# A windowed attention and gated expert kernel: another opening for TensorE's instruction stream, another order in the first six steps, and one batch for the last four rows

## The chip, the cores and the metric

The kernel runs on one core of a Trainium2 chip. The metric is the device time of one execution in microseconds. Of the kernel before, three executions were timed: 4324.14, 4325.08 and 4339.78 us, with the median 4325.08. The profile comes from a further execution.

Five engines work side by side, each with its own instruction stream: PE (TensorE, matrix multiplies; PEld is its loading of weights), DVE (VectorE), ACT (ScalarE), POOL (GpSimd) and SP (SyncE, which here issues the transfers). They wait for each other through semaphores.

## The reference

The input `x` is two images of 128 channels and 256 x 256 pixels in 32-bit floats. Cut to what matters, the reference computes:

```python
x = x + conv_ref(ln_c(x))        # attention in windows of 8 x 8 pixels
t = to_tokens(x)                 # one token of 128 channels per pixel
t = t + ffn_ref(ln_t(t))         # experts
x = from_tokens(t, x)

# conv_ref: q, k, v by one 128 -> 384 product; each 8 x 8 window of q looks at
# a 12 x 12 window of k and v; relative position terms from q; a fixed mask
# that leaves one pixel in four; softmax; an output product
# ffn_ref: gate = softmax(x @ router_w + router_b); the best 2 of 8 experts,
# their gates divided by their sum; sum of gate * (x @ expert_w[e] + expert_b[e])
```

The mask parts the pixels into four parity planes (even and odd rows and columns) that have nothing to do with each other in the attention. `ln_c` and `ln_t` norm every pixel over its 128 channels.

## The kernel before

**Tiles.** Channels lie on the 128 partitions. The images are cut into 64 strips of 8 image rows (32 to an image). A strip has four planes, 512 pixels each, and four "rows" of two image rows, also 512 pixels each. A row (i, k) is row k of strip i.

**Steps.** One loop runs over n (L811). Step n computes the attention of plane n (strip n // 4), prepares plane n + 1, and does the experts for rows of the strip before. There are 256 planes; the loop has 263 turns, the last seven of which only drain the experts. The pieces of a step are generators, and the loop body takes one portion of a generator at a time: the order of the calls in the body is the order of the instructions on each engine. Inside `tc.manual_schedule` nothing is moved.

- `scores` (L464): products of `keys` with `au` (position terms, L476), then of `kcol` with `qs` (L493), then the exponential on ACT (L501).
- `attend` (L505): the sums of the exponentials (L514), called "the sums" here, the weighted values `av` (L524), and on DVE `sT`, `rc`, `rT` and `o` (L534 to L544), which divide.
- `out_project` (L548): `po` (L552) from `o`, and `xv` (L557), which adds it to the plane in place.
- `project` (L399), called `ahead` in the loop: values `pv` (L349) and `pu` (L408), the transposes and shifts that make `au` (L385 to L412), `pk` (L422) with ACT's copies to `kcol` (L433, L443), and `pq` (L447) with ACT's copy to `qs` (L449).
- `norms` (L565): ACT squares a row (L576), PE sums it over the channels in `plt` (L582), DVE works out the inverse deviation. It serves two rows at once: f, whose experts follow, and c, a row of a later strip (`row_at`, L761) that is to be normed for the attention. From n = 249 on there is no c, and the steps 250 to 255 are called short.
- `route` (L608): DVE picks two of eight gates per pixel. `spread` (L650): DVE's transpose makes `gT`, and SP sends it to a memory tile `gd` in two transfers (L661).
- `Experts`: `fetch` (L682) brings one expert's gates, spread over all partitions, in a transfer of 256 KB into one of eight `gb` tiles; `fetch_means` brings the mean term `sb`; `means` (L701) forms `xs`; `times` (L707) multiplies by a gate on DVE or POOL to give `xe`; `product` (L716) adds one expert's matrix product to `acc`; `end` (L722) adds `acc` to the row. `store` (L749) writes the row out.
- `first_norms` (L282) does the statistics of the first seven rows before the loop, in groups of four and three, and `ln1` (L273) norms them.

**Rooms.** Products go through three banks `ps_mm`, one bank `ps_acc` for `acc`, and four banks `ps_att` for the attention. The pool `xpool` has six strips.

**Instructions of PE.** `nc.tensor.addr_align(256, offset=157)` (L825) stands ahead of the scores of every step from 6 to 255. It asks for empty instructions until the next one has slot 157 of a block of 256. With `max_nops=0` the same call gives a branch over the space instead. PE fetches its program in blocks of 256 instructions; these fetches appear in the trace as the traffic of an instruction queue. A float32 product is four instructions, two loads of weights and two multiplies; a transpose is two.

**The start.** The loads of the first two strips are issued first, then the weights. Then DVE and PE prepare the weights: means taken off, four transposes `pw` (L166), the relative position tables (L176 to L190) and their product `wrel` (L195). Behind these in the order come the first statistics (L292), the projections of plane 0, and the loop.

Of the kernel before, what the change touches and what calls it, by code (L numbers as in the profile page):

```python
# [19 lines left out]
E = 8  # L20
# [23 lines left out]
KR, KC = 6, 10  # L44
NK = KR * KC
SLOT = 64
BLOCK, FIRST_LIMIT = 256, 99
NU = 9


@with_exitstack
def kernel(
# [39 lines left out]
    def mm_tile(name):  # L92
        return ps_mm.tile([P, 512], F32, tag="mm", name=name)

    def ctile(shape, name):
        return const.tile(shape, F32, tag=name, name=name)


    nc.scalar.preload_act_table_set("natural_log_exp_and_others")


    strips = [(b, s) for b in range(B) for s in range(NS)]
# [2 lines left out]
    def load_x(i, k, paced=False):  # L105

        if i >= len(strips):
            return
        b, s = strips[i]
        if k == 0:  # L110
            xt[i] = xpool.tile([P, R, W], F32, tag="xt", name=f"xt{i}")
        r = s * R + 2 * k
        if paced:
            nc.scalar.copy(xt[i][:, 2 * k, 0:1], onesm[:, 0:1])
        nc.sync.dma_start(xt[i][:, 2 * k : 2 * k + 2, :], x[b, :, r : r + 2, :])
# [22 lines left out]
    for j in range(4):  # L138
# [14 lines left out]
    nc.sync.dma_start(ew, expert_w.rearrange("e d c -> d e c"))  # L153
    nc.sync.dma_start(eb, expert_b.rearrange("e c -> (e c)").partition_broadcast(P))
    load_x(2, 0)

    wmean = ctile([P, 3, 1], "wmean")
    nc.vector.tensor_reduce(wmean, wall[:, 0:3, :], AX.X, ALU.add)
    nc.vector.tensor_scalar_mul(wmean, wmean, 1.0 / C)
    nc.vector.tensor_tensor(  # L160
        wall[:, 0:3, :], wall[:, 0:3, :], wmean.broadcast_to([P, 3, P]), ALU.subtract
    )
    wt = ctile([P, 4, P], "wt")
    pw = mm_tile("pw")
    for j in range(4):
        nc.tensor.transpose(pw[:, j * P : (j + 1) * P], wall[:, j, :], ident)  # L166
    nc.vector.tensor_copy(wt.rearrange("p j c -> p (j c)"), pw)
    nc.vector.tensor_scalar_mul(wt[:, 0, :], wt[:, 0, :], SCALE)
    wq, wk, wv, wo = (wt[:, j, :] for j in range(4))

    relT = []
    for rname, rsb in zip(("relh", "relw"), relsb):
        pr = mm_tile(f"p_{rname}")
        nc.tensor.transpose(  # L176
            pr[:, :n_rel], rsb.rearrange("r h d -> r (h d)"), ident[:n_rel, :n_rel]
        )
        rT = ctile([P, n_rel], f"{rname}T")
        nc.vector.tensor_scalar_mul(rT, pr[:, :n_rel], SCALE)  # L180
        relT.append(rT)
    mid = n_rel // 2
    lo = mid - 2 * (PR - 1)
    relbd = ctile([P, P], "relbd")
    nc.gpsimd.memset(relbd, 0.0)
    for h in range(HEADS):
        hp = slice(h * DH, (h + 1) * DH)
        for j in range(2):
            c0 = h * DH + NU * j
            nc.vector.tensor_copy(  # L190
                relbd[hp, c0 : c0 + NU], relT[j][hp, lo : lo + 2 * NU - 1 : 2]
            )
    wrel = ctile([P, P], "wrel")
    pr = mm_tile("p_wrel")
    nc.tensor.matmul(pr[:, :P], lhsT=wall[:, 0, :], rhs=relbd, start=True, stop=True)  # L195
    nc.vector.tensor_copy(wrel, pr[:, :P])

    xn, vwin, vrows, kcol = [], [], [], []
    zero = ctile([P, KR, P], "zero")
# [362 lines left out]
    for g in gboth:  # L562
        nc.gpsimd.memset(g, 0.0)

    def norms(f, c, nm):  # L565

        g = gboth[next(g_turn) % len(gboth)]  # L570
        srcs = []
        for j, src in ((0, f and rows_of(*f)), (2, c and ln1_src(*c))):
            if src is None:
                continue
            sq = work.tile([P, CH], F32, tag=f"sq{j}", name=f"sq{j}{nm}", bufs=1)
            nc.scalar.activation(sq, src, AF.Square)  # L576
            srcs += [(j, src), (j + 1, sq)]
        yield
        plt = mm_tile(f"plt{nm}")
        for j, src in srcs:  # L580
            for t in range(NT):
                nc.tensor.matmul(  # L582
                    plt[32 * t : 32 * t + 32, :P],
                    lhsT=rw[:, j],
                    rhs=src[:, t * P : (t + 1) * P],
                    start=(j == srcs[0][0]),
                    stop=(j == srcs[-1][0]),
                )
        yield
        plg = mm_tile(f"plg{nm}")  # L590
        nc.vector.transpose(plg[:, :P], plt[:, :P])
        p4 = plg[:, :P].rearrange("p (t e) -> p t e", e=32)
        k0, k1 = (0 if f else 1), (2 if c else 1)
        r, u = rstd(p4, plg[:, P : P + 2 * NT], k0, k1, nm)
        rs = None
        if f:
            rs = small.tile([P, NT], F32, tag="rs", name=f"rs{nm}")
            nc.vector.scalar_tensor_tensor(rs, u[:, 0], 3.0, r[:, 0], ALU.add, ALU.mult)
        if c:
            nc.vector.scalar_tensor_tensor(  # L600
                g[:, 1, :, 1], u[:, 1 - k0], 3.0, r[:, 1 - k0], ALU.add, ALU.mult
            )
        yield g, rs, p4
# [121 lines left out]
    class NoExperts:  # L725
# [18 lines left out]
        def end(self):  # L744
            pass

    to_store = []

    def store(i, k):  # L749
# [5 lines left out]

    n_planes = 4 * len(strips)

# [9 lines left out]

    first = [(0, k) for k in ln_rows(0)] + [row_at(n) for n in (-2, -1) if row_at(n)]
    parts = [first_norms(first[j : j + 4], f"n{j}") for j in range(0, len(first), 4)]
    for _ in range(3):
        for part in parts:
            next(part)
    if len(strips) > 1:
# [31 lines left out]

    ET = mybir.EngineType
    with tc.manual_schedule(engines={ET.PE, ET.DVE, ET.Activation, ET.Pool, ET.SP}):  # L810
        for n in range(n_planes + 7):  # L811
            i, pl = divmod(n, 4)
            score, attn, outp, ahead, norm, rout = none, none, none, none, none, none
            if n < n_planes:
                score = scores(n, states[n])
                attn = attend(n, states[n])
                outp = out_project(n, states[n])
            if n + 1 < n_planes:
                states[n + 1] = {}
                ahead = project(n + 1, states[n + 1])  # L820

            if 6 <= n < n_planes:
                nc.tensor.addr_align(BLOCK, offset=BLOCK - FIRST_LIMIT)  # L825


            next(score, None)
            new, row = NoExperts(), None
            if gated and gated[0]:  # L830
                rout = route(*gated[0], *gated[2])
            next(rout, None)
            nxt.fetch(5, nc.scalar)
            for _ in rout:
                pass
            next(score, None)
            next(ahead, None)
            nxt.fetch(7, nc.scalar)
            if gated:
                f, c, made = gated  # L840
                gd = spread(f, c, made[0], f"_{n}")
                new = Experts(*f, gd) if f else new
            if n + 1 < n_planes:
                send_values(n + 1, states[n + 1]["sent"])
            if gated and c:
                row = (*c, fetch_rstd(gd, f"_{n}"))
            next(ahead, None)
            if n + 1 < n_planes:
                states[n + 1]["shift"]()
            next(ahead, None)  # L850
            next(ahead, None)
            for e in (4, 6, 7, 5):
                ex.product(e)


            f = (i - 1, pl) if 0 < i <= len(strips) else None
            c = row_at(n)
            if f or c:
                norm = norms(f, c, f"_{n}")
            next(norm, None)  # L860
            next(attn, None)
            nxt.means()
            new.fetch_means()
            if n + 1 < n_planes:
                take_values(n + 1)
            for e in (0, 1, 2, 3):
                nxt.times(e, dve)
            new.fetch(0, dve)
            for e in (4, 6):
                nxt.times(e, dve)  # L870
            new.fetch(1, dve)
            ex.end()
            new.fetch(2, dve)
            next(attn, None)
            next(attn, None)


            ex = nxt
            next(norm, None)
            load_x((n + 9) // 4, (n + 9) % 4, paced=True)  # L880
            new.fetch(3, dve)
            while to_store:
                store(*to_store.pop())
            next(ahead, None)
            ex.product(0)
            made = next(norm, None)
            ex.product(1)
            ex.product(2)
            new.fetch(4, nc.scalar)
            nxt.behind(6)  # L890
            nxt.times(5, pool)
            if row:
                ln1(*row, pool)
            if pl == 3 and i + 2 < len(strips):
                halo(i + 2)
            nxt.times(7, pool)
            if n + 2 < n_planes:
                borders(n + 2)
            next(outp, None)
            ex.product(3)  # L900
            next(outp, None)
            new.fetch(6, dve)
            gated, nxt = (f, c, made) if made else None, new
            states.pop(n, None)

def shape_constants():

# [56 lines left out]
```

## Time and profile before

| | |
|---|---|
| median of three executions | 4325.08 us |
| profiled execution, its own time | 4331.68 us |
| its span, first to last instruction | 4329.9 us |
| mean granted clock of PE | 0.991 |
| busy: PE, DVE, ACT, POOL | 97%, 88%, 30%, 25% |
| first statistics on PE (L292) begin | 11.67 us |
| keys of step 0, of step 6, of step 7 begin | 28.71, 124.89, 143.88 us |
| median of a step from 7 to 248 | 16.24 us |
| keys of step 249, of step 255 begin | 4122.65, 4239.45 us |
| last `xv` (L557, step 255) begins | 4253.34 us |
| empty instructions, all ahead of keys | 8123 |

The times in the table are read from the timeline, which lists each engine's work in the order of its start. A step is taken from the start of its keys on PE (L476) to that of the next. In the busy table a share is of the span. In the stretches' table each row is one piece of time with the busy time of each engine in it and the mean granted clock of PE; 1.00 is the full clock. An idle time is shown in brackets, with what ended it; "issue" means that the profile shows no engine or transfer that was waited for.

### The profile page before, as it was taken

How to read it: one execution, taken by the hardware profiler on the slowest of the kernel's cores; microseconds unless marked ns; L12 is line 12 of the kernel's file. 1: busy time of each engine (PE TensorE's matmuls, PEld its weight loads, DVE VectorE, ACT ScalarE, POOL GpSimd, SP SyncE). 2: the span in 40 equal slices, each digit the busy share in tenths (PEclk: the TensorE clock that was granted, in tenths of full speed). 3: DMA queues.
4: the chain of work that ended last, by engine and by line, in shares of the span. 5: the costliest groups of instructions: out<-in, count | busy, mean ns of one | idle time of the engine just before them, and what ended most of it. 6: DMA issues, size and time to landing. Idle time of an engine off the chain costs nothing. (4 is left out here: it accounts for less than half of the span.)

```text
span 4329.9 us, 224393 instructions
## 1 busy us (share of the span) xinstructions
PE 4220.6 (97%) x94273; PEld 2464.3 (57%) x94273; DVE 3790.8 (88%) x11850; ACT 1320.4 (30%) x3774; POOL 1087.9 (25%) x1126
## 2 busy tenths in 40 slices
PE   7899999999999999999999999999999999999987
PEld 5455555555555555555555555555555555555553
DVE  5798898898888889988889889898888898888877
ACT  3223333332333333233332333333323232333321
POOL 1222222222222222222222222222222222222211
PEclk9999999999999999999999999999999999999999
DMA  4787878788787877878788787887878788787865
GB/s 112 212 245 241 248 236 246 241 244 248 235 239 240 247 236 248 248 235 251 240 247 241 243 247 238 247 248 239 247 233 246 233 250 244 239 246 239 245 190 190
DMA packets 824578, 1022.17 MB, mean 236 GB/s; under 512 B 137634, under 2 KB 409634, under 8 KB 823594
## 3 DMA queue, kind: packets, MB, share of 16 engines
q1 hardware_dynamic: 822864, 1007.52, 76.5%
q8 instruction: 769, 12.60, 1.3%
q14 instruction: 215, 1.76, 0.1%
q10 hardware_dynamic: 730, 0.29, 0.0%
HBM read 863.78 MB, written 143.75 MB: 233 GB/s over the span
## 5 line engine op out<-in xcount | busy, mean ns | idle before, releaser
L716 PE MATMUL acc<-xe,ew 128*128 128x512 f32 x4096 | 1918.4, 601 | 20.7 <-DVE gb L690 14.5
L716 PEld LDWEIGHTS acc<-xe,ew 128*128 128x128 f32 x4096 | 758.4, 190 | 940.3 <-issue 872.7
L707 DVE TENSOR_TENSOR xe<-xs,gb 128x512 f32<-128x512 f32 x1536 | 950.4, 685 | 11.2 <-PE acc L716 1.6
L711 POOL COPY last<-xe 128x1 f32<-128x1 f32 x256 | 47.6, 186 | 3120.0 <-DVE gb L690 3110.9
L707 POOL TENSOR_TENSOR xe<-xs,gb 128x512 f32<-128x512 f32 x512 | 652.1, 1275 | 1.5 <-PE att L524 1.0
L493 PE MATMUL att<-qs,kcol 32*60 32x32 f32 x32768 | 395.3, 223 | 16.7 <-issue 15.9
L493 PEld LDWEIGHTS att<-qs,kcol 32*60 32x60 f32 x32768 | 390.3, 127 | 21.1 <-issue 20.5
L275 POOL TENSOR_TENSOR xn<-xt,rb 128x512 f32<-128x512 f32 x249 | 374.0, 1502 | 93.5 <-DMA rb<-gd 92.7
L524 PEld LDWEIGHTS att<-pT,vwin 64*32 64x32 f32 x32768 | 349.7, 105 | 47.2 <-issue 9.3
L524 PE MATMUL att<-pT,vwin 64*32 64x32 f32 x32768 | 348.4, 200 | 6.5 <-issue 5.5
L501 ACT ACTIVATE pT<-att 128x1024 f32<-128x1024 f32 x256 | 262.2, 1024 | 296.3 <-PE att L493 296.3
L349 PE MATMUL pv<-wt,xn 128*128 128x128 f32 x2048 | 301.9, 291 | 0.9 <-issue 0.9
L412 DVE STREAM_TRANSPOSE uT<-pu 128x512 f32<-128x512 f32 x256 | 183.5, 717 | 132.1 <-PE pu L408 127.2
L576 ACT ACTIVATE sq<-xt 128x512 f32<-128x512 f32 x505 | 292.6, 630 | 0.0
L396 DVE STREAM_TRANSPOSE au<-auT 128x512 f32<-128x512 f32 x256 | 269.7, 1053 | 9.0
L552 PE MATMUL po<-o,wt 128*128 128x512 f32 x512 | 266.4, 602 | 10.2 <-DVE o L544 6.6
L408 PE MATMUL pu<-xn,wrel 128*128 128x512 f32 x512 | 267.5, 604 | 0.9 <-issue 0.9
L433 ACT COPY kcol<-pk 128x560 f32<-128x560 f32 (+2 forms) x344 | 183.4, 533 | 276.5 <-PE pk L422 273.7
L422 PE MATMUL pk<-xn,wt 128*128 128x512 f32 (+2 forms) x528 | 261.9, 580 | 0.0
L447 PE MATMUL pq<-xn,wt 128*128 128x512 f32 x512 | 261.7, 592 | 0.0
L349 PEld LDWEIGHTS pv<-wt,xn 128*128 128x128 f32 x2048 | 252.3, 194 | 11.7 <-issue 1.3
L476 PEld LDWEIGHTS att<-au,keys 32*64 32x64 f32 x8192 | 118.2, 133 | 230.2 <-PE po L552 183.8
(2437 smaller groups left out, 4853.9 us busy)
## 6 DMA issues: line engine op xcount, KB each, us to landing
gb<-gd SPq DMA_DIRECT2D x2048, 256.0 KB, 5.7
vwin<-vrows SPq DMA_DIRECT2D x512, 240.0 KB, 5.1
xt<-in_x_dram SPq DMA_DIRECT2D x256, 256.0 KB, 6.6
sb<-gd SPq DMA_DIRECT2D x256, 256.0 KB, 4.5
out_dram<-xt SPq DMA_DIRECT2D x256, 256.0 KB, 6.0
rb<-gd SPq DMA_DIRECT2D x249, 256.0 KB, 3.5
vrows<-vr SPq DMA_DIRECT2D x168, 256.0 KB, 3.9
vrows<-vr SPq DMA_DIRECT2D x160, 128.0 KB, 3.7
```

The lines of the kernel that those rows point to most:

```text
L275: eng.tensor_tensor(xn[i % 2][:, :, :, k, 1 : PC + 1], ln1_src(i, k).rearrange("p (y j x) -> p y x j", y=2, x=2), rb.rearrange("p (y j x) ...
L349: nc.tensor.matmul(pv[:, j * P : (j + 1) * P], lhsT=xp[:, k, 1 : PC + 1], rhs=wv, start=True, stop=True,)
L396: nc.vector.transpose(au.rearrange("p m a s -> p a s m"), auT[n % 2])
L408: nc.tensor.matmul(pu, lhsT=wrel, rhs=inner, start=True, stop=True)
L422: nc.tensor.matmul(pk[:, : m * PC], lhsT=wk, rhs=xp[:, part[0] : part[0] + m, 1 : PC + 1], start=True, stop=True,)
L493: nc.tensor.matmul(sc[rows, h, 32 * t : 32 * t + 32], lhsT=kk[hp, half * HP + t, 0:NK], rhs=qs[hp, m0 : m0 + 2].rearrange("p m a s -> p (m ...
L501: nc.scalar.activation(pT, att[:, :, 0:HQ], AF.Exp)
L524: nc.tensor.matmul(av[hp, half, 32 * t : 32 * t + 32], lhsT=vv[rows, t, hp], rhs=pT[rows, h, 32 * t : 32 * t + 32], start=True, stop=True,)
L552: nc.tensor.matmul(po, lhsT=wo, rhs=state["o"].rearrange("p f z -> p (f z)"), start=True, stop=True)
L576: nc.scalar.activation(sq, src, AF.Square)
L707: eng.tensor_tensor(self.xe[e], self.xs, self.gb.pop(e), ALU.mult)
L716: nc.tensor.matmul(self.acc, lhsT=ew[:, e, :], rhs=self.xe.pop(e), start=(e == 0), stop=not self.xe)
```

## The change

Five things change.

1. A branch to slot 51 of a block stands at the opening of PE's program.
2. The squares, sums and copy of the first group of rows (first portion of `parts[0]`) come ahead of the preparation of the weights; the rest of the statistics comes behind it. The lines of the preparation are the same; they stand in the diff below right after `next(parts[0])`.
3. In steps 0 to 5 (`FILL`), the portions of `ahead` with `pk` and `pq` are taken behind the sums over the channels (`plt`) and not ahead of the sums. `plt` then lies in the accumulators' bank.
4. The filling to slot 157 ahead of the scores remains for the steps 7 to 249. Step 6 and the short steps fill to slot 40 ahead of the sums, behind the products of the experts 4, 6, 7, 5.
5. The loop has 256 turns. In place of the seven draining turns, `finish_last` takes the three rows under way and the last four. Row (62, 3) is routed as before. The four rows of strip 63 go through one tile of sums over the channels and one chain of DVE operations, for the statistics and the gates of all four. POOL makes all eight `xe` of row (62, 2), and for later rows but the last those of experts 2 and 5; DVE makes the rest. The gates of four rows are fetched into rooms of `xpool`, two rooms of four gates to a row, those of row (63, 1) into `gb` tiles; each row's products go to a bank of the attention's room.

```diff
-BLOCK, FIRST_LIMIT = 256, 99
+BLOCK, FIRST_LIMIT, SUMS_AT = 256, 99, 40
 NU = 9
+FILL = 6
...
     nc.scalar.preload_act_table_set("natural_log_exp_and_others")
+    nc.tensor.addr_align(BLOCK, offset=51, max_nops=0)
...
     parts = [first_norms(first[j : j + 4], f"n{j}") for j in range(0, len(first), 4)]
-    for _ in range(3):
+    next(parts[0])
...
+    for part in parts[1:]:
+        next(part)
+    for _ in range(2):
         for part in parts:
             next(part)
...
-        for n in range(n_planes + 7):
+        for n in range(n_planes):
...
-            if 6 <= n < n_planes:
+            usual = n > 6 and row_at(n - 1) is not None
+            if usual:
                 nc.tensor.addr_align(BLOCK, offset=BLOCK - FIRST_LIMIT)
...
-            next(ahead, None)
-            next(ahead, None)
+            filling = n < FILL
+            if not filling:
+                next(ahead, None)
+                next(ahead, None)
             for e in (4, 6, 7, 5):
                 ex.product(e)
+            if n >= 6 and not usual:
+                nc.tensor.addr_align(BLOCK, offset=SUMS_AT)
...
             if f or c:
-                norm = norms(f, c, f"_{n}")
+                room = None
+                if filling:
+                    room = ps_acc.tile([P, 512], F32, tag="acc", name=f"plt_{n}")
+                norm = norms(f, c, f"_{n}", room)
...
             next(norm, None)
+            if filling:
+                next(ahead, None)
+                next(ahead, None)
             load_x((n + 9) // 4, (n + 9) % 4, paced=True)
...
+        finish_last(ex, nxt, gated)
```

The new function, cut to its order:

```python
def finish_last(ex, nxt, gated):
    rows = [(len(strips) - 1, k) for k in range(4)]
    ...
    for _ in route(*f, *made):            # row (62, 3)
        pass
    nxt.fetch(5, nc.scalar)
    nxt.fetch(7, nc.scalar)
    ...
    gd = spread(f, None, made[0], "_c")
    fetch_all(0, gd)                      # its nine fetches, into an xpool room
    for e in (4, 6, 7, 5):
        ex.product(e)
    plt = mm_tile("plt_l")
    ...
    nxt.means()
    ex.end()
    for e in (0, 1, 2, 3, 4, 6, 5, 7):
        nxt.times(e, nc.gpsimd)
    for e in (0, 1, 2, 3, 4, 6, 5, 7):
        nxt.product(e)
    ...
    gds = []
    for r in range(4):
        ...
        for k in (1, 0):
            nc.sync.dma_start(to[k], gT[:, r, k])
        if r == 1:
            fetch_all(1, gds[0])
    store(*to_store.pop())
    fetch_into(2, gds[1], [...])          # into gb tiles
    accs = ps_att.tile([P, 4, CH], F32, tag="att", name="accs")
    todo = [f] + rows
    before = nxt
    for row, at in enumerate(todo):
        xes = multiply(at, row)
        if row < 2:
            fetch_all(row + 3, gds[row + 2])
        if row == 0:
            before.end()
            store(*to_store.pop())
        else:
            src = rows_of(*todo[row - 1])
            nc.vector.tensor_add(src, accs[:, (row - 1) % 4], src)
            store(*todo[row - 1])
        products(accs[:, row % 4], xes)
    ...
```

## The prediction

> **What bounds the kernel now.** I read the busy table and its slices first, to see where TensorE is not full.
>
> ```profile
> PE 4220.6 (97%) x94273; PEld 2464.3 (57%) x94273; DVE 3790.8 (88%) x11850; ACT 1320.4 (30%) x3774; POOL 1087.9 (25%) x1126
> ...
> PE   7899999999999999999999999999999999999987
> ```
>
> TensorE is busy 97% of the span; only the first two slices and the last two (108 us each) have a gap. The change touches just these, so the steady steps are no subject. Second, the table of stretches (columns: stretch, its length, busy time of PE, PEld, DVE, ACT, POOL, granted clock, DMA share, GB/s).
>
> ```profile
> 99.30:124.90 25.60, 9.92 (x355) 6.93 (x354) 14.15 (x57) 5.16 (x14) 1.49 (x1) 0.77 0.47 135
> ...
> 4180.50:4200.30 19.80, 17.08 (x351) 9.79 (x351) 14.66 (x46) 4.25 (x12) 2.98 (x4) 0.90 0.61 180
> ...
> 2000.00:2016.30 16.30, 16.30 (x370) 9.56 (x369) 14.74 (x47) 5.02 (x14) 4.74 (x5) 1.00 0.80 242
> ```
>
> A steady step is 16.3 us and all PE. Step 5 takes 25.6 us with 9.9 us of PE work, and a short step near the end takes 19.8 us with fewer instructions than a steady one, at a clock of 0.90. Third, the timeline of PE says what it waited for (start, duration, work, and in brackets the idle time before).
>
> ```profile
> 55.84 0.31 PE L582 MATMUL plt<-sq,rw 128*32 128x128 f32 x1 [2.26 <-issue]
> ...
> 69.21 1.67 PE L552 MATMUL po<-o,wt 128*128 128x512 f32 x2 [2.19 <-DVE o L544]
> ...
> 124.89 1.16 PE L476 MATMUL att<-au,keys 32*64 32x128 f32 x32 [13.93 <-issue]
> ...
> 4187.20 3.59 PE L716 MATMUL acc<-xe,ew 128*128 128x512 f32 x8
> 4190.72 0.66 PE L514 MATMUL att<-pT,ones 64*32 64x256 f32 x16
> ...
> 4200.30 1.16 PE L476 MATMUL att<-au,keys 32*64 32x128 f32 x32 [2.72 <-issue]
> ...
> 4262.77 9.71 PE L716 MATMUL acc<-xe,ew 128*128 128x512 f32 x16 [4.98 <-DVE gb L690]
> ...
> 4318.53 7.13 PE L716 MATMUL acc<-xe,ew 128*128 128x512 f32 x16 [1.83 <-DVE xt L722]
> ```
>
> "Issue" ahead of L476 is the fill: empty instructions that PE's sequencer steps through. Two hundred of them lie between 109.97 and 124.83, so 74 ns each. Step 2 waits 2.19 us for `o` from DVE, and runs `po` after it in 1.67 us for 1.02. The last rows come every (4318.53 - 4262.77) / 5 = 11.15 us, with products of 7.13 us when the clock is full.
>
> **The fill counts** follow from PE's order of instructions and the limit of 256 (for the kernel before this gives the 8123 empty instructions that the trace has). Before: 201 ahead of step 6, 47 ahead of 7, 30 ahead of 8, 31 in each up to 249, 63 at 250 and 251, 67 at 252 to 255. After: a branch at the opening, 6 ahead of the sums of step 6, none at 7, then 30 and 31 as before, 94 ahead of the sums of 250, 67 in 251 to 254, 91 in 255. Steps 8 to 249 keep their slots, fills and order: zero, hidden or not.
>
> **Opening: weights behind the first statistics.** PE's statistics start at 11.67 now, behind `wrel`, though x has landed by about 4.2 us. The weights' transposes (0.75 us) then come later; they issue no DMA, so the order in SP's queue stays. What ends last is the DVE chain of `xn`; I estimate step 0 at 27.1 instead of 28.7: gain 1.6 (0 to 4). The branch itself is not in the trace. The Trainium skill, "Runtime: NRT & Kernel Launch", Instruction fetch mechanics, says that a taken branch outside the two loaded pages forces a fetch before execution goes on, which speaks against it. The nearest row: the next block comes about 4.1 us after the entry of the one before; PE does nothing before 7.57, so I take 0 (0 to 4).
>
> **Steps 0 to 5.** Without the fill they take now 15.98 + 13.40 + 12.73 + 14.50 + 13.95 + (25.63 - 14.86) = 81.3. The change takes `pk` (1.08) and `pq` (0.95) out of the chain keys, scores, pv, pu, sums, av, `o`, `po` and puts them in the wait for `o`: av to `po` is 2.8 us, with 0.3 to 0.9 of `plt` in it. So 2.0 us a step, 12 in all, and the half clock that follows the wait, 1.7 us in each of five steps, 8.5 more: 61 us. The same page calls the crossing of a block "mostly hidden"; here PE stood for 0.91, 2.26, 0.93, 0.17 and 2.58 us at such borders, 6.85 us in all, so the measurement decides. The new phase puts 16 borders between the sums of step 0 and the products of step 6, and 16 x 4.1 = 66 us is a floor under them. As borders lie unevenly, I walked each step's pieces against the fetch times: 15 + 10 + 11.8 + 12.8 + 10.3 + 12 = 72 us. Gain 9.3 (0 to 18). Behind the moved `pk` and `pq` on ACT lie the copies to `kcol` and `qs` that the next scores need; `po` (0.86) and keys (0.46) hide the last copy (0.9); uncovered it costs 0.9 a step. `plt` in the accumulators' bank waits for nobody, as no expert runs before step 5.
>
> The clock is the other weighing. Row: granted clock 0.5 for 3.41 us from 42.28, 55.94, 69.59, 83.24, 96.9, each after an idle PE of only 2.2 us. "TensorE: Matmul & The Clock Gate", Part 1, lets the clock drop after an idle window of about 3.4 us. By the rule, the waits of 2.2 us cost no clock, and a cure of them gains 12, not 20; by the row, an idle left of 0.9 us at `o` plus fetch stalls of 1 to 2 us may still fall in such a window. I keep 2 us (0 to 8) as a loss for that.
>
> **Steps 6 and 7.** The fill of step 6 goes from 201 to 6: 14.8 us. The fill of 7 (34 of its 47 lay bare, 141.3 to 143.8): 2.5. The clock was half for 17.07 us from 113.96; 12 us of this beside work from 124.9 on, in which step 6 took 18.98; take 2 (0 to 4). Opening in all: 1.6 + 9.3 - 2 + 14.8 + 2.5 + 2 = 28.2.
>
> **Short steps 250 to 255.** Ahead of keys, 50 to 53 of the empty instructions lay bare, PE idle 2.7 to 2.9 us each, with the clock at half for 3.41 us afterwards (4141.69, 4162.17, 4182.65, 6.83 from 4199.72): `pu` 1.92 for 1.02. Ahead of the sums, the sequencer has run ahead: PE has a queue of `pu`, `pk`, `pq` and 3.5 us of products before it. The fetch that its crossing starts began at 4187.04, while the matrix unit reached that product at 4188.91, so the sequencer would be at the sums near 4185.2, 5.5 us before they run. 67 x 74 ns = 4.96 is hidden; 94 are 6.96, bare by 1.5. Uncovered, 67 cost 5.0 a step. Steps 249 to 254 now take 18.29 + 19.58 + 19.96 + 19.82 + 20.81 + 18.34 = 116.8; with no bare fill I take 15.8 + 5 x 16.3 (the steady step, as DVE's 14.7 and PE's 16 lie under it) + 1.5 = 98.8. Gain 18.0. In 255 nothing is projected, and the 91 (6.7 us) have some 3.4 us of products as cover: bare 3.3, less 2.2 of half clock and of waiting for DVE: -1.1. Together 16.9.
>
> **Last rows.** From the `xv` of step 255 (4253.34) to the end there are 76.6 us now. Then: row (62,3) is routed alone, its `gT` at 4257.6 as now; `plt_l` ends near 4259; one chain on 128x16 and 128x128 elements, twenty-odd operations of 0.2 to 1.2 us behind the route (3.6) and its waits for ACT, ends near 4269. POOL meanwhile makes row (62,2)'s eight products' inputs at 1.25 us. SP then issues the first two `gd` (0.52 and 0.59 each half) and waits for the first: 4271.5 + 4.2 (issue to landing as at 4302.77) puts the first fetch of row (63,0) near 4274.4. The store of (62,1) and the fetches of later rows stand behind that wait in SP's queue; the store has 40 us to spare. Each row is nine fetches of 0.78 us (337 GB/s at best), 7.0, against 7.13 of products and 6 x 0.65 + 0.7 of DVE: 7.0 to 7.7 a row in place of 11.15. Row (63,0)'s last gate is there at about 4284, three more rows make 4306, then a product, L722 (0.69) and 3.5 from there to the end: 4311 to 4313. The accumulators' four banks are those of the attention, free since 4253; the new tile's clearing lies on POOL at the start, idle there. Gain 17.5 (0 to 24).
>
> **The sum.** 28.2 + 16.9 + 17.5 = 62.6. The profiled execution (4331.68; span 4329.9, so 1.8 lies outside) would be 4269; it stands 6.6 above the median of 4325.08, for which I forecast 4325.1 - 62.6 = 4262.5. A measurement of this kernel tells about 0.5% (21.6 us) from no change.
>
> **The rivals.**
> Fetch-bound opening: reordering gains nothing, since the sequencer waits for blocks however the pieces lie; only the two fills count, 17.3 instead of 28.2: 4273. For it: 16 x 4.1; against: the floor is 66, not 81.
> Fill at the sums not hidden: no gain in the short steps, and 51 more empty instructions x 74 ns = 3.8 lost: 4325.1 - 28.2 - 17.5 + 3.8 = 4283. For it: a normal fill is hidden only because a wait for `o` released the sequencer early; against: the fetch at 4187.04.
> Tail bound by latency: the batch makes four rows wait for the longest chain, and the fetch of 45 gates queues behind two `gd` landings; gain nothing: 4280. For it: a row's chain (gT to gates) was partly overlapped already; against: idle of 3 to 5 us ahead of every other row.
> Slower: the new phase of the instruction blocks in steps 8 to 249, one mechanism: if the opening branch shifts the blocks so that a fetch shows in each of 242 steps, 62.6 / 242 = 0.26 us a step eats the gain, and 0.35 us makes it 0.5% slower; a typical stall of 0.9 would give 4480. Against: 31 fills and slot 157 are the same, and steps took 16.24 with these.
>
> **How the numbers follow.** Main course 0.62, opening 0.12, fill 0.10, tail 0.11, slower 0.03, and 0.02 for partial sums of the middle three, which would still end near 4300 to 4310. The predicted time is the main course's. Low end: opening 35, short steps 20, tail 24 make 4246; high end: two half failures, 4290. Faster: all but the last two, 0.94; same 0.03; slower 0.03.
>
> **What would show it.** Right: step 0 near 27 us, step 6 near 101, step 7 near 116 and no long idle for issue there; no idle for issue ahead of keys in steps 250 to 255, which take 16.3, with 7940 empty instructions in all; the last five rows' products 7.0 to 7.7 us apart, and 59 us from the last `xv` to the end. Wrong: idle for issue at new borders in steps 1 to 5, idle ahead of L514 in the short steps, half clock in the same places, rows waiting for gates by more than 2 us each, or steady steps off 16.24.

## The result, and the profile after

The changed kernel took 4294.98 us, the median of four executions (4291.43 to 4302.19), against 4324.61 of the kernel before on the same chip: a ratio of 0.993, with a 95% interval of 0.9908 to 0.9951. That is 29.6 us less. The forecast was 62.6 less, 4262.5, with a range up to 4290: the sign was right, the size twice too large, and the time lies outside the range.

The busy table, the PE row of its slices and the queue of PE's instructions (packets, MB, share), of the kernel after:

```profile
PE 4214.7 (98%) x94273; PEld 2457.6 (57%) x94273; DVE 3786.3 (88%) x11752; ACT 1315.5 (31%) x3750; POOL 1093.2 (25%) x1125
...
PE   7999999999999999999999999999999999999997
...
q8 instruction: 769, 12.60, 1.3%
```

PE's work is the same number of products. The second slice is full now and the one before the last too; the first and the last are still at 7.

The table of stretches of the kernel after (stretch, length, busy time of PE, PEld, DVE, ACT, POOL, granted clock, DMA share, GB/s): steps 0, 3, 5 and 6, and the short steps 250 and 252.

```profile
26.70:40.90 14.20, 12.02 (x345) 7.30 (x344) 8.31 (x18) 5.25 (x15) 0.00 (x0) 1.00 0.36 96
...
63.60:76.10 12.50, 9.57 (x337) 6.23 (x336) 6.52 (x18) 3.70 (x8) 2.06 (x2) 1.00 0.37 107
...
88.40:101.30 12.90, 11.41 (x353) 7.65 (x352) 9.31 (x33) 4.58 (x11) 1.31 (x1) 0.87 0.43 115
101.30:123.30 22.00, 15.56 (x367) 9.53 (x367) 14.54 (x49) 5.30 (x16) 4.32 (x5) 0.84 0.57 193
...
4124.00:4145.20 21.20, 19.19 (x359) 10.59 (x358) 15.12 (x48) 4.41 (x12) 2.96 (x4) 0.84 0.67 218
...
4160.60:4176.40 15.80, 15.63 (x351) 9.03 (x350) 14.48 (x46) 4.14 (x12) 2.96 (x4) 1.00 0.70 216
```

Step 5 is 12.9 us where it was 25.6, and a short step 15.8 where it was 19.8, at the full clock. But step 6 takes 22.0, and step 250 takes 21.2, both at a clock of 0.84.

The timeline of PE after (start, duration, work, and in brackets the idle time before) says why:

```profile
36.18 0.29 PE L485 MATMUL att<-pT,vwin 64*32 64x32 f32 x15 [1.49 <-issue]
...
39.88 1.12 PE L513 MATMUL po<-o,wt 128*128 128x512 f32 x2 [0.69 <-ACT kcol L404]
...
42.95 0.94 PE L454 MATMUL att<-qs,kcol 32*60 32x32 f32 x72 [0.71 <-issue]
...
72.05 0.28 PE L485 MATMUL att<-pT,vwin 64*32 64x32 f32 x12 [2.62 <-issue]
...
100.26 1.12 PE L513 MATMUL po<-o,wt 128*128 128x512 f32 x2 [0.19 <-DVE plg L552]
...
102.80 0.32 PE L437 MATMUL att<-au,keys 32*64 32x128 f32 x2 [0.81 <-issue]
...
108.45 0.41 PE L454 MATMUL att<-qs,kcol 32*60 32x32 f32 x3 [4.06 <-issue]
...
4134.99 0.67 PE L475 MATMUL att<-pT,ones 64*32 64x256 f32 x16 [1.85 <-issue]
...
4217.64 0.67 PE L475 MATMUL att<-pT,ones 64*32 64x256 f32 x16 [4.03 <-issue]
...
4247.52 9.53 PE L767 MATMUL accs<-xel,ew 128*128 128x512 f32 x16 [6.44 <-DVE xel L760]
4261.28 9.47 PE L767 MATMUL accs<-xel,ew 128*128 128x512 f32 x16 [4.23 <-DVE xt L878]
4272.24 7.13 PE L767 MATMUL accs<-xel,ew 128*128 128x512 f32 x16 [1.49 <-DVE xt L878]
4280.87 7.13 PE L767 MATMUL accs<-xel,ew 128*128 128x512 f32 x16 [1.49 <-DVE xt L878]
4289.39 7.13 PE L767 MATMUL accs<-xel,ew 128*128 128x512 f32 x16 [1.39 <-DVE xt L878]
```

The wait of 2.2 us for `o` has gone: PE is idle ahead of `po` for 0.19 us in step 5 and for 0.30 to 1.21 in the others, in the first three steps 0.7 until ACT has made `kcol`. In its place PE stands at borders of instruction blocks: 2.62 us in step 3, 4.06 in the scores of step 6. Two counts say that these are borders. Between the waits that end at 36.18 and 42.95, and between those that end at 102.80 and 108.45, lie 127 and 128 loads of weights with as many multiplies, so about 256 instructions. And the queue q8 moved 769 packets; all loads, multiplies and empty instructions of PE (2 x 94273 + 7940) are 767.5 times 256. The sums of steps 250 and 255 still wait for their fills, and each of the last rows waits for an addition on DVE (L878).

Set side by side, the two profiled executions (4329.9 and 4300.4) differ by 29.5 us, and the stages add up to that within 0.1:

| stage | before | after | gain | forecast |
|---|---|---|---|---|
| start to keys of step 0 | 28.7 | 26.7 | 2.0 | 1.6 |
| steps 0 to 5, with the fill of step 6 | 96.2 | 74.6 | 21.6 | 22.1 |
| step 6, with the fill of step 7 | 19.0 | 21.9 | -2.9 | 4.5 |
| steps 7 to 248 | 3978.8 | 3985.0 | -6.2 | 0 |
| steps 249 to 254 | 116.8 | 99.8 | 17.0 | 18.0 |
| keys to last `xv` of step 255 | 13.9 | 16.9 | -3.0 | -1.1 |
| last `xv` to the end | 76.6 | 75.5 | 1.1 | 17.5 |

Two stages failed, the last rows by 16.4 us and step 6 by 7.4. The steady steps have the same instructions in both kernels. Over all kernels of this study, whatever their change, the stretch from step 7 to step 249 took from 3962.5 to 3987.3 us, most steps 16.24 and a few 17 to 19; so the 6.2 us in this pair say nothing of the change, and stages are compared below rather than whole times where only a few microseconds are at stake. Stages scatter too: seven kernels, the changed one among them, have the same last rows, and their time from the last `xv` to the end is 74.7 to 77.0 us.

### The profile page after: what moved, and what is told of

It is laid out like the page before. It is cut to its first block, busy times and chain, and to the rows that moved or that the text cites. A ratio compares the mean times of both kernels' runs of the same rounds, so it can differ in the third digit from the quotient of the medians.

```text
span 4300.4 us, 224047 instructions
## 1 busy us (share of the span) xinstructions
PE 4214.7 (98%) x94273; PEld 2457.6 (57%) x94273; DVE 3786.3 (88%) x11752; ACT 1315.5 (31%) x3750; POOL 1093.2 (25%) x1125
## 3 DMA queue, kind: packets, MB, share of 16 engines
q1 hardware_dynamic: 822864, 1007.52, 75.7%
## 4 chain that ended last, share of the span: by engine, by line
PE 97%; issue 1%; DVE 1%; DMA 1%; SPq 0%; ACT 0%; POOL 0%; POOLq 0%; DVEq 0%
PE acc L677 41%; PE att L454 8%; PE att L485 7%; PE pv L310 7%; PE plt L543 6%; PE pu L369 5%; PE po L513 5%; PE pk L383 5%; PE pq L408 5%; PE att L437 4%; PE att L475 3%; DMA gl<-gd_l 1%; PE accs L767 0%; PE pltn L253 0%; DMA xt<-in_x_dram 0%
## 5 line engine op out<-in xcount | busy, mean ns | idle before, releaser
L677 PE MATMUL acc<-xe,ew 128*128 128x512 f32 x4016 | 1880.8, 599 | 10.2 <-issue 8.9
L677 PEld LDWEIGHTS acc<-xe,ew 128*128 128x128 f32 x4016 | 740.9, 190 | 913.0 <-issue 856.3
L668 DVE TENSOR_TENSOR xe<-xs,gb 128x512 f32<-128x512 f32 x1500 | 927.6, 685 | 8.6
```

The lines of the kernel that those rows point to most:

```text
L668: eng.tensor_tensor(self.xe[e], self.xs, self.gb.pop(e), ALU.mult)
L677: nc.tensor.matmul(self.acc, lhsT=ew[:, e, :], rhs=self.xe.pop(e), start=(e == 0), stop=not self.xe)
```

## The experiments

Two theories stood against each other. By the first, the stages of the two profiles are to be believed: the opening gives some 20 us, the short steps 17, the batch of the last rows nothing. By the second, each part gives what was forecast, and something else takes half of it back.

**One part undone at a time.** `old_tail`:

```diff
-        for n in range(n_planes):
+        for n in range(n_planes + 7):
...
-        finish_last(ex, nxt, gated)
```

> The changed kernel with the loop of 263 turns and no batch for the last rows; all else as changed. Theory A (the batch gives next to nothing: in the two profiles the time from the last xv to the end is 76.6 us before and 75.5 after): about 4296, 75 to 79 us from the last xv to the end. Theory B (the batch gives the forecast 17.5 and the loss lies elsewhere, as in the steady steps): about 4312.

Measured: 4297.94 (4290.69 to 4308.38), a ratio to the kernel before of 0.993 (0.9909 to 0.9952), as with the batch. From the last `xv` to the end: 78.5 us. Theory A holds: the batch, some 160 lines of the change, is worth 0 to 3 us.

`old_start` has the opening of before:

```diff
-    nc.tensor.addr_align(BLOCK, offset=51, max_nops=0)
...
-FILL = 6
+FILL = 0
...
-            usual = n > 6 and row_at(n - 1) is not None
+            usual = n >= 6 and row_at(n - 1) is not None
```

and the weights stand ahead of the first statistics.

> The changed kernel with the opening of before: no branch, the weights ahead of the first statistics, pk and pq ahead of the sums in steps 0 to 5, step 6 filled ahead of its scores. Theory A (in the profiles step 7 begins 20.6 us earlier after the change): about 4315.6, keys of step 7 near 144. Theory B (the opening gave the forecast 28.2, lost again later): 4323.

Measured: 4315.75, ratio 0.9974 (0.9965 to 0.9984); keys of step 7 at 146.4. So the opening is worth about 20 us, two thirds of the whole gain, and theory A holds.

`old_short` fills ahead of the scores in the short steps:

```diff
-            usual = n > 6 and row_at(n - 1) is not None
+            usual = n > 6
```

> The changed kernel with the fill of steps 250 to 255 ahead of the scores, as before. Theory A (the fill ahead of the sums is hidden but for its ends): steps 250 to 254 take 19.5 to 20.8 again, 17 us more, 4312. Theory B (the fill bare ahead of the scores only moved the waiting of DVE): within 5 us of the changed kernel's 4295.

Measured: 4315.53, ratio 0.9966 (0.995 to 0.9982); steps 250 to 254 took 19.5, 19.9, 19.8, 20.8 and 18.4, those of before within 0.1. Theory A holds.

**The opening taken apart.** `fill0` moves `pk` and `pq` back:

```diff
-FILL = 6
+FILL = 0
```

> The changed kernel with pk and pq ahead of the sums in steps 0 to 5 again; plt in the usual bank. Theory A (moving them gives the forecast 9.3 us, the wait for o and the half clock come back): keys of step 6 near 110.6 instead of 101.3, 4304. Theory B (the fetch of instruction blocks sets these steps, and only the order of the waits changes): keys of step 6 within 3 us of 101.3, 4295 to 4298.

Measured: 4297.31, ratio 0.9934 (0.9912 to 0.9956), keys of step 6 at 107.6. By the time as a whole this is theory B; the stage lies between the two. On the same chip, with the move, step 0 to step 6 took 75.7 and 77.3 us (`old_tail`, `old_short`), without it 81.0: the move gives about 4.5 us here. The timeline of PE in this run:

```profile
106.61 1.10 PE L513 MATMUL po<-o,wt 128*128 128x512 f32 x2 [1.75 <-DVE gb L651]
...
115.23 0.41 PE L454 MATMUL att<-qs,kcol 32*60 32x32 f32 x3 [4.61 <-issue]
```

The wait ahead of `po` is back (1.75; DVE gives `o` here too, the name is that of its next operation). In return the block borders cost only 0.48 us before step 6, against 8.1 after the change (1.49, 0.71, 0.79, 2.62, 1.20, 1.30): the wait for `o` had covered the fetches of blocks. The half clock is back too, once in each of steps 0 to 4 (from 40.12, 53.78, 67.43, 81.08 and 94.74). The 4.61 us in step 6 stay, so the move has no part in them.

`fill_only`, `no_branch`, `own_banks`, `psum_stats` and `no_fill255` were timed once each, so their stages are read and not their whole times. `fill_only` has the weights ahead of the statistics in addition:

```diff
-FILL = 6
+FILL = 0
...
-    next(parts[0])
...
-    for part in parts[1:]:
+    for part in parts:
         next(part)
```

> The changed kernel with both reorderings of the opening undone (weights first, pk and pq ahead of the sums); the branch and the new fills remain. Theory A (the fill is most of the opening's gain, the reorderings give 1.6 and about 5): keys of step 0 near 28.5, of step 7 near 131 to 132 in place of 122 to 129. Theory B (fetch stalls give the reorderings nothing): step 7 within 1 us of the run with pk and pq alone moved back, 130, less what other runs of the same day have.

Measured: keys of step 0 at 28.7, of step 6 at 112.1, of step 7 at 134.6; 4300.82 in all. Theory A's sign is right. Beside the run named `best2`, on the same chip and with both reorderings (26.5, 102.4, 124.0), the statistics give 2.2 us and the move 7.5. On one chip it was 4.5, on the other 7.5; four kernels with the move on a third chip took 78.6 to 81.7 us from step 0 to step 6, with no run there without it. So the move's gain is known only roughly: 81.7 with it is more than the 81.0 of `fill0`. The fills and the branch alone, without the reorderings, give 12.8 us up to step 6: 83.3 from step 0 here, 96.2 in the kernel before.

`no_branch`:

```diff
-    nc.tensor.addr_align(BLOCK, offset=51, max_nops=0)
```

> The changed kernel without the branch at the opening. The order of instructions then puts 247 empty instructions ahead of the sums of step 6 in place of 6. Theory A (74 ns each, little cover as no products run there yet): idle for issue of 12 to 17 us ahead of the sums of step 6, keys of step 7 13 to 18 us later, from both the branch costing nothing. Theory B (the stalls at block borders are what the step has anyhow): less than 8 us later.

The timeline of PE:

```profile
109.97 0.44 PE L453 MATMUL att<-qs,kcol 32*60 32x32 f32 x10 [5.14 <-issue]
...
131.56 1.11 PE L474 MATMUL att<-pT,ones 64*32 64x256 f32 x16 [16.14 <-issue]
```

Keys of step 7 came at 140.9, 16.9 later than in `best2`. Theory A holds: the branch is what saves the long fill. Its own cost does not show: in the kernel after it is one instruction of 0.30 us at 0.8 us, when PE has no product before 5.21, and the keys of step 0 came at 27.1 without it, and at 26.5 to 28.1 with it and the statistics first.

**The last rows taken apart.** Two suspects are in the timelines of the kernel after. The first is the wait for L878 that was shown. The sums of products of all rows lie in one tile of four banks, and each row's products begin 0.05 us after the addition of the row before has ended (4280.14 + 0.68, then 4280.87), though that reads another bank. `own_banks` gives each row a tile:

```diff
-        accs = ps_att.tile([P, 4, CH], F32, tag="att", name="accs")
+        accs = {}
...
-                nc.vector.tensor_add(src, accs[:, (row - 1) % 4], src)
+                nc.vector.tensor_add(src, accs[row - 1], src)
...
-            products(accs[:, row % 4], xes)
+            accs[row] = mm_tile(f"accl{row}")
+            products(accs[row], xes)
```

> The changed kernel with a tile of one bank for each of the last five rows' sums of products, in place of one tile of four banks. Theory A (PE waits at each row for DVE's addition of the row before, although that lies in another bank: 1.4 to 1.5 us idle ahead of the last three rows): this idle goes, rows 7.2 apart, from the last xv to the end 71 in place of 75.5 us. Theory B (gates or DVE's multiplications end last all the same): 75 us, another idle of 1.4 us ahead of each row.

The timeline of PE:

```profile
4243.71 16.81 PE L767 MATMUL accl<-xel,ew 128*128 128x512 f32 x32 [6.44 <-DVE xel L760]
...
4272.32 12.28 PE L767 MATMUL accl<-xel,ew 128*128 128x512 f32 x28 [0.55 <-DVE xel L760]
```

Two rows' products now stand in one line with no gap. From the last `xv` to the end: 67.4 us, 8.1 less, more than the 4.5 of theory A, since the first two rows joined too. What PE waits for now is the next input (L760). The chain of waits of the changed kernel shows where these 8 us lie. It runs through the transfers of gates up to 4277, and through L878 only behind that:

```profile
4251.88 5.95 DMA gl<-gd_l
...
4271.66 5.47 DMA gl<-gd_l
...
4280.21 0.61 DVE xt L878
```

`own_banks` leaves the gates where they were: SP issues those of the last row from 47.2 us behind the last `xv` on, and from 46.8 in the changed kernel. The gain comes behind them, 20.3 us to the end in place of 28.7.

The second suspect is in DVE's timeline of the kernel after:

```profile
4232.59 0.17 DVE L807 SCALAR_TENSOR_TENSOR u_l<-u_l,plg_l 128x16 f32<-128x16 f32 x1
4232.79 0.98 DVE L808 TENSOR_SCALAR u_l<-u_l 128x16 f32<-128x16 f32 x1
...
4235.03 1.19 DVE L812 TENSOR_TENSOR u_l<-u_l,r_l 128x16 f32<-128x16 f32 x1
4236.25 1.19 DVE L813 SCALAR_TENSOR_TENSOR rs_l<-u_l,r_l 128x16 f32<-128x16 f32 x1
...
4238.81 0.29 DVE L821 TENSOR_REDUCE mx_l<-lg_l 128x16 f32<-128x128 f32 x1
```

and in POOL's:

```profile
4230.03 9.87 POOL L668 TENSOR_TENSOR xe<-xs,gb 128x512 f32<-128x512 f32 x8 [10.72 <-DMA gb<-gd]
```

Operations of one size take 0.17 us with an operand in PSUM (`plg_l`), and up to 1.19, the length of one POOL multiplication (9.87 / 8 = 1.23), with both in SBUF, while POOL multiplies. `psum_stats` puts `u` and the logits into PSUM:

```diff
-        u, r_, rs, mx, sd = (
+        r_, rs, mx, sd = (
...
+        room_l = mm_tile("room_l")
+        u = room_l[:, 0:m]
...
-        nc.vector.tensor_tensor(u, r_, r_, ALU.mult)
-        nc.vector.scalar_tensor_tensor(u, u, -1.0, p4[:, :, E + 1], ALU.mult, ALU.add)
+        nc.vector.tensor_tensor(mx, r_, p4[:, :, E], ALU.mult)
+        nc.vector.scalar_tensor_tensor(u, mx, -1.0, p4[:, :, E + 1], ALU.mult, ALU.add)
...
-        lg = small.tile(by_e, F32, tag="lg_l", name="lg_l", bufs=1)
+        lg = room_l[:, P : 2 * P].rearrange("p (q e) -> p q e", e=E)
```

> The changed kernel with the intermediate values of the last four rows' statistics (u and the logits) in a PSUM bank in place of SBUF, as the steps have them; no arithmetic is changed. Theory A (DVE's small operations with only SBUF operands wait for POOL's multiplications beside them: 1.19 us for the same 128x16 operation that takes 0.17 otherwise): none above 0.35 us beside POOL, the chain from plt_l to gT_l 10 in place of 15.1 us, from the last xv to the end 70.5. Theory B (these small operations are slow by their shape): chain 15 us, 75.5.

DVE's timeline of this run:

```profile
4225.59 0.18 DVE L814 TENSOR_TENSOR room_l<-room_l,r_l 128x16 f32<-128x16 f32 x1
...
4229.60 2.17 DVE L839 TENSOR_TENSOR cmp_l<-cmp_l,ties 128x1024 f32<-128x1024 f32 x1
```

The same operation takes 0.18 us in place of 1.19: not the shape, the place of the operands. But the chain shortens to 12.6, not 10 us, and the stage to 72.2, 3.4 less in place of 5. The gates of the last row are issued from 44.5 us behind the last `xv` on, 2.3 earlier. The large comparisons, both operands in SBUF, now come while POOL still multiplies: this one takes 2.17 where it took 1.23 behind POOL's end, and POOL's eight take 11.78 us in place of 9.87.

`no_fill255`:

```diff
-            if n >= 6 and not usual:
+            if n >= 6 and not usual and n != 255:
```

> The changed kernel without the 91 empty instructions of step 255. Theory A (4.0 us of them lie bare): from the keys to the xv of step 255 13.4 in place of 16.9 us. Theory B (DVE or the clock holds the sums up as well): 16 us.

Measured: 13.4 us from keys to `xv`. Theory A holds: beside the 16.9 of the changed kernel, the fill of 91 cost 3.5 us. The size is rough: other kernels with this fill took 15.2 to 17.9 us there, and the two below without it 14.0 and 15.3.

`best` has all three.

> All three together: own banks, statistics in PSUM, no fill in step 255. If each theory A holds and they add: from the last xv to the end 66.3 us, step 255 13.4, in all 12.6 us less than the changed kernel, 4282. If the gates' fetch sets the rows: 69 to 71 us, 4286.

Measured: 4277.74 (4269.31 to 4279.5), ratio 0.9892 (0.9867 to 0.9918). Step 255 took 14.0 us, and from the last `xv` to the end 65.0 passed: 10.5 less than the changed kernel, where the two edits alone gave 8.1 and 3.4. They add but for a microsecond.

`best2` parts the fill of step 250:

```diff
             if usual:
                 nc.tensor.addr_align(BLOCK, offset=BLOCK - FIRST_LIMIT)
+            elif n > 6 and row_at(n - 2) is not None:
+                nc.tensor.addr_align(BLOCK, offset=BLOCK - FIRST_LIMIT - 32)
```

> The three changes of the run named best, and the 94 empty instructions of step 250 parted: 31 ahead of its scores, as in a steady step, and 63 ahead of its sums. If only what exceeds some 67 lies bare and makes the clock fall: step 250 15.8 to 16.3 in place of 19.6 to 22.1, 4273. If the first fill of a short step is bare in any place: 4278, as the run named best.

Measured: 4265.78 (4259.14 to 4269.65) against 4317.44 of the kernel before on that chip, ratio 0.9882 (0.9863 to 0.9902). Step 250 took 16.4 us; its idle for issue ahead of the sums fell from 1.85 to 0.23, and the clock stayed full. The first line is of step 250, the second of step 251:

```profile
4113.78 0.67 PE L475 MATMUL att<-pT,ones 64*32 64x256 f32 x16 [0.23 <-issue]
...
4130.60 0.67 PE L475 MATMUL att<-pT,ones 64*32 64x256 f32 x16 [0.85 <-issue]
```

A part of the gain went to step 251, which took 17.1 us in place of 15.4: together the two steps took 33.5 us, 3.0 less than in the changed kernel. As a whole the step from `best` to `best2` lies within the intervals of both; the stage shows it. In the last rows the chain of waits of `best2` runs through the fetch of gates from 4223 to 4239, and from 4240.70 on through PE's products without a gap up to the last addition:

```profile
4228.48 5.75 DMA gd_l<-gT_l
...
4234.30 5.02 DMA gl<-gd_l
```

The stage takes 63.2 us there, with the same code of the last rows as `best` (65.0). The forecast 59.1 was not reached.

## Why the prediction was wrong, point by point

- **Statistics first:** 1.6 forecast, 2.0 in the pair of profiles, 2.2 between two runs on one chip. Right; the branch at no cost, too.
- **Steps 0 to 5:** 72 us and 2 for the clock forecast, 74.6 measured. The mechanism was right on both sides: the wait for `o` went, and block borders took a part of it back. The forecast gain with the clock's term (9.3 - 2) was 7.3; 6.7 was measured in the profiles, 4.5 and 7.5 by experiment. The clock took about 1.5 of its 2 us: the first five steps ran at 1.00, step 5 at 0.87 (`pv` 2.08 for 1.16, `pu` 1.57 for 1.02). Not foreseen were the waits that are left ahead of `po`, 3.8 us in the six steps; the forecast looked for ACT's copies only ahead of the scores.
- **Fill of step 6:** 14.8 forecast. Right: `no_branch`, with 247 empty instructions there, is idle for 16.1 us.
- **Step 6 failed.** A gain of 4.5 was forecast, 2 from the clock and 2.5 from the fill of step 7; the step became 2.9 longer. Both terms were read too large. "12 us of this beside work" is 6.1: the half clock of before ended at 131.03, and work began at 124.89. And PE was idle for 1.57 us, not 2.5, ahead of the keys of step 7, as the timeline of before has it:

```profile
143.88 0.70 PE L476 MATMUL att<-au,keys 32*64 32x128 f32 x32 [1.57 <-issue]
```

What turned the sign is a term that stood in the forecast with nothing: the block borders inside step 6. Before, with slot 157 at the keys, PE never waited for issue between the keys of step 6 and the fill of step 7. Now one border lies at the last keys and the next three multiplies ahead of the end of the scores. PE works off the 256 instructions between in 1.6 us (102.80 to 104.39), and the next block is not there. PE stood there for 3.5 to 5.8 us in every run with the new fills, with and without reordering (5.1 without the branch, ten multiplies ahead of the end), and not with the old opening. With 0.81 and 0.89 us at two other borders this is 5.8 us in the profile, and the clock fell to half beside it (`pv` 2.08 for 1.16, `pu` 1.70 for 1.02). I had walked the borders only to the keys of step 6, and took the rest of the step as before. The 4.1 us that I took for a fetch was too short as well: from the end of one such wait to the end of the next, one block further, it was 6.8 us (36.18 to 42.95), 6.7 (72.05 to 78.71) and 5.7 (102.80 to 108.45). In the first two PE had enough to do or to wait for in this time and stood only 0.71 and 1.20 us for the block. So the fetch is not slower in step 6 than ahead of it; why it takes longer than 4.1 us at these places stays open.
- **Short steps:** 18.0 forecast, 17.0 measured. The mechanism was right: ahead of the sums of steps 251 to 254 PE is idle for issue for 0.43 us at most. That the number is so near is luck, since two errors cancel: the steps took 15.4 to 15.9, less than the 16.3 I took, and step 250, whose 94 I had bare by 1.5, was bare by 1.85, but the clock fell as well, and its products of 2.84 us took 5.25. The step cost 5 us more than a short step.
- **Step 255:** a mis-sized term, -1.1 forecast and -3.0 measured. The bare 3.3 was near (4.0 idle, worth about 3.5); the relief of 2.2 that I set against it did not come.
- **The last rows failed.** Two of their terms did. "One chain ... ends near 4269", 15.7 us behind the last `xv`, ended 21.3 behind it. Its operations were taken at 0.2 to 1.2 us with no wait for another engine's work in SBUF; beside POOL's multiplications, operations with SBUF operands alone took up to seven times as long. Seven of them (L806, L808, L811 to L813, L820, L822) took 6.5 us together, and 1.5 in `psum_stats`: these 5.0 us are nearly all of the 5.6 that the chain was late. POOL's work was in the same paragraph, and I did not ask what the two share. At the gates 2.7 us of this were left, since SP went from the first `gd` to the first fetch in 2.6 us (4246.14 to 4248.69) and not in 4.2: this fetch of row (63, 0) came 23.8 us behind the last `xv` where 21.1 was forecast, and that of the last row 22.3 us later, as forecast (three times 7.0 to 7.7). The larger failure is "7.0 to 7.7 a row in place of 11.15", which took each row's products to run while its gates arrive, and gave nothing for a wait on the row before. Some 14 of the 16.4 missing us came in behind the fetches of gates. The last rows are 8.5 to 8.6 apart, 7.13 of products and 1.4 to 1.5 of waiting for DVE's addition, since I took four banks of one tile for four rooms; and the first two are 13.8 and 11.0 apart, with the clock at half behind idle PE (9.5 for 7.13). Together the rows took 41.9 us from the first one's products to the last one's, where four times 7.0 to 7.7, 28 to 31, was forecast. With tiles of one bank (`own_banks`) 8.1 us of this go. With both causes taken away (`best`) the stage is 10.5 us shorter. What the other 6 us are was not tried.

The count of empty instructions, 7940, came out as forecast. Three small sums of the prediction are off: 4271.5 + 4.2 is 4275.7 and not 4274.4, the short steps with step 255 have 59 empty instructions more and not 51, and the chances of a faster kernel add up to 0.95.

The rival that the tail gives nothing was forecast at 4280, from the longest chain and the fetches behind the `gd` landings. Its time for this stage was right. Its reason was so only in part: the chain was 5.6 us late, and the chain of waits does run through the fetches, but they kept their forecast spacing, and half of the loss went with the shared tile. Taken with the shortfalls of steps 6 and 255 it leads to 4289; most of the rest up to the measured time are the 6.2 us by which the steady steps of the pair differ. The range allowed for two such half failures, to 4290, but not for one whole one and one half.

## What to carry to other kernels

A batch that replaces serial work has its own chain and its own rooms: before counting its gain, ask for each operation which engine works beside it on the same memory, and for each room whether the parts are tracked apart. When filling is moved in an instruction stream, walk the block borders to the first step that is aligned again, not to the step where the edit ends. A step whose wait is taken away may have been hiding a fetch in it.

## What the runs showed of the hardware that was not expected

- DVE and POOL hold each other up over SBUF, even for tiny operations: 1.19 us for 16 elements a partition beside POOL's multiplications, 0.18 with one operand in PSUM. The Trainium skill, "GPSIMD Engine Reference", Specifications, says that POOL's interface to SBUF is shared with DVE, and that DVE instructions in a two-port mode or with two SBUF inputs contend. The runs agree, and give the size: such an operation took up to 1.0 us longer, where one POOL multiplication takes 1.23, and POOL's own eight take 11.78 in place of 9.87 us when DVE's large comparisons run beside them. A reduction with one input in SBUF (L821) took 0.29 us beside POOL, no more than with this input in PSUM. The TENSOR_SCALAR with one (L808) took 0.98 in place of 0.18; whether it runs in a two-port mode no run here shows.
- The clock does not follow the length of an idle time alone. In the kernel before, 2.19 to 2.58 us of idle, ahead of `po` or at a block border, went with half clock in each of five steps; after the change PE stood 2.62 us at 72.05, and the step ran at 1.00. All half-clock stretches of a run begin whole multiples of 3.41 us apart (before: 42.28, 55.94, 69.59, 83.24, 96.90, each four times 3.41 behind the last; after: 91.53 and 105.18). On this grid the 2.62 us fall on both sides of a border, 1.62 ahead of 71.05 and 1.00 behind. But the grid does not explain everything either: 1.30 us of idle inside one stretch (90.06 to 91.36, after) went with a fall at its end, and 1.75 inside another (108.11 to 109.86, before) did not. What decides stays open. "TensorE: Matmul & The Clock Gate", Part 1, calls the window free-running, which fits the grid; its idle window of about 3.4 us is more than these traces needed.
